# Spread one-hots made per batch between two message products, in a graph network layer on one core

## Chip, cores and metric

The kernel runs on one core of a Trainium2 chip. The metric is the device time of one execution in microseconds. A core has five instruction queues: PE (matmuls; PEld is its weight load), DVE (vector), ACT (scalar), POOL (which here issues the gathers) and SP (which only issues transfers). Each queue runs its instructions in the order written; semaphores hold an instruction until what it needs is done.

## The reference

One message passing layer with 1250 nodes of 512 features (a vector part of 3 x 128 and a scalar part of 128) and 40000 edges, sorted by their target node, followed by a residual sum and a layer norm:

```
s_j        = silu(x[src, 384:] @ W1 + b1) @ W3 + b3            # per edge, 384 wide
edge_basis = (rbf(r) * cutoff(r)) @ W2 + b2                     # 20 radial functions
s1, s2, s3 = split(s_j * edge_basis)                            # 128 each
v_msg      = v_j * s1[:, :, None] + s3[:, :, None] * edge_attr[:, None, :]
x          = x + segment_sum(concat(v_msg, s2), dst)
...        # per node: v@U, v@U@V, norms, a two-layer network, products -> rows
x          = x + segment_sum(rows[src], dst)
out        = layernorm(x0 + x)
```

The change concerns the term `s3 * edge_attr`: three vector components of an edge are the same 128 numbers, each times one of the edge's three attributes.

## The kernel before

**Tiles.** Edges come in 79 chunks of 512. A group is four chunks (16 tiles of 128 edges); there are 20 groups. A batch is one tile of each of the four chunks of a group: 4 batches a group, 80 batches, numbered t, with t = 4g + i. The last group is not full: its batches have 3, 2, 2 and 2 tiles. The targets of a chunk lie in a window of 32 nodes, so summing edges into nodes is a matmul with a one-hot matrix of 128 edges x 32 nodes. `hot` (line 759) has these one-hots of a group. `spread` (line 769) has each one-hot three times, times the edge's three attributes, so that `s3 * edge_attr` is summed by matmuls and never formed.

**A step of the main loop** (lines 1352 to 1370; step t):

- `messages(t)` (line 813): DVE multiplies the gathered table rows with the edge factors `eb`, which lie in PSUM: line 819 makes the part for s2 and s3 (1024 elements a partition for four tiles), line 820 the vector part (1536). The result `msg` has two buffers.
- `make_pair(t)` (line 834): DVE compares, for the count of links that the second sum needs.
- `run(first, t)`: single tasks of PE and ACT.
- `add_messages(t - 1)` (lines 851, 858): PE sums batch t-1 into `agg`, 4 matmuls with `hot` and 12 with `spread` (each recorded as two). `count_links(t - 1)` (line 876) follows.
- `run(early, t)`, then `edge_factors(t + 1)` (line 806): PE makes `eb` of the next batch in PSUM. There is one `eb` buffer, so this waits for line 820 of batch t.
- `gather(t + 3)` (line 700): POOL issues one indirect DMA for each tile, 128 rows of 2560 bytes. The first of them is also made to wait for `edge_factors(t + 1)`. Four `rows_t` buffers.
- `run(late, t)`, then `run(dve, t)`: single tasks of DVE, in an order set by a table.

The tables `first`, `early`, `late` and `dve` are written by hand, by step and rank; they repeat every eight steps (two groups). The tasks on DVE behind the pair are, by t mod 8 in the repeating part:

| t mod 8 | DVE tasks behind the pair, by line |
|---|---|
| 0 | 1046, 1052 (scaled rows of a node block), 911 (counts) |
| 1 | 948, 953 (sums of a block), 732 (basis arguments) |
| 2 | 920, 925 (counts), 761 (`make_hot`), 743 (`make_basis`) |
| 3 | 774 (`make_spread`), 743 |
| 4 | 774, 958 (residual), 911 |
| 5 | 1070 (a part of a row), 761, 722 (basis arguments) |
| 6 | 774, 1067 (a part of a row) |
| 7 | 774, 920, 925, 728 (basis arguments) |

Each line 774 makes half a group's spread: 8 tiles x 3 x 32 = 768 elements a partition. A group's spread has two buffers of 16 tiles. The first group's two halves are made in step 0 behind the pair.

**Around the loop.** Before it, node features are loaded, the table for the gathers is computed and written, and the edges' data are turned; the first gather starts 33 us into the span. While the loop runs, blocks of nodes whose sums are complete go through the second half of the layer, and PE begins products of the second sum (line 1118). The last L819 starts at 461.8 us; then the second sum and the layer norm are finished.

Of the kernel before, what the change touches and what calls it, by code (L numbers as in the profile page):

```python
# [10 lines left out]
F32 = mybir.dt.float32  # L11
# [9 lines left out]
P = 128  # L21
# [14 lines left out]
CPG = 4  # L36
SHARE = 16
MARGIN = 8
WIN = SHARE + 2 * MARGIN
# [23 lines left out]
def gnn_resnorm(  # L63
# [276 lines left out]
    with tc.If(misses_v == 0) as in_windows:  # L340
        windowed(tc, sh)
# [199 lines left out]
def windowed(tc, sh):  # L541
# [14 lines left out]
    NB, NGR, NCH, width = sh.NB, sh.NGR, sh.NCH, sh.width  # L556
# [4 lines left out]
    EPG = TPC * CPG  # L561
# [4 lines left out]
    def lanes(g, i, j):  # L566

        c = g * CPG + j
        if c >= NCH:
            return 0  # L570
        n = CHUNK if c < NCH - 1 else last_rows
        return max(0, min(P, n - i * P))


    batches = [(g, i) for g in range(NGR) for i in range(TPC) if lanes(g, i, 0)]
    NT = len(batches)

    def tiles(g, i):
        return [j for j in range(CPG) if lanes(g, i, j)]

    def runs(g, i):

        out = []
        for j in tiles(g, i):
            if out and lanes(g, i, out[-1][-1]) == lanes(g, i, j):
                out[-1].append(j)
            else:
                out.append([j])
        return [(slice(js[0], js[-1] + 1), len(js), lanes(g, i, js[0])) for js in out]
# [4 lines left out]
    def last_tile(g, j):  # L594
        return max(i for i in range(TPC) if lanes(g, i, j))
# [14 lines left out]
    with tc.tile_pool(name="msg", bufs=4) as pool, tc.tile_pool(  # L610
        name="rbf", bufs=1
# [77 lines left out]
        rows_of, msgs, onehots, turned, hots, spread = {}, {}, {}, {}, {}, {}  # L689
# [76 lines left out]
            )  # L766
            hots[g] = hot

        def make_spread(g, half):
            if half == 0:  # L770
                spread[g] = pool.tile([P, EPG, 3, WIN], F32, name="spread", bufs=2)
            n = EPG // 2
            at = slice(half * n, (half + 1) * n)
            nc.vector.tensor_mul(  # L774
                spread[g][:, at],
                hots[g][:, at, None, :].to_broadcast([P, n, 3, WIN]),
                sh.attr[:, g, at, :, None].to_broadcast([P, n, 3, WIN]),
            )
# [22 lines left out]
        def edge_factors(t):  # L801
            g, i = batches[t]
            eb = ps_work.tile([P, CPG, BANK], F32, name="eb")
            for j in tiles(g, i):
                rows = slice(j * FEAT, j * FEAT + N_RBF + 1)
                made = nc.tensor.matmul(  # L806
                    eb[:, j, :V], turned[g][rows, i, :], sh.w2_sb[rows, :],
                    start=True, stop=True,
                )
            ebs[t] = eb  # L810
            return made

        def messages(t):
            g, i = batches[t]
            eb, rows_t = ebs.pop(t), rows_of.pop(t)

            msg = pool.tile([P, CPG, V + 2 * C], F32, name="msg", bufs=2)
            for js, n, m in runs(g, i):
                nc.vector.tensor_mul(msg[:m, js, V:], rows_t[:m, js, V:], eb[:m, js, C:V])  # L819
                nc.vector.tensor_mul(  # L820
                    msg[:m, js, :V].rearrange("p t (k c) -> p t k c", k=3),
                    rows_t[:m, js, :V].rearrange("p t (k c) -> p t k c", k=3),
                    eb[:m, js, None, :C].to_broadcast([m, n, 3, C]),
                )
            msgs[t] = msg

        def make_pair(t):

            g, i = batches[t]
            pair = pool.tile([P, CPG, PARTS * WIN], F16, name="pair", bufs=2)  # L830
            for js, n, m in runs(g, i):
                e = g * EPG + i * CPG + js.start
                shape = [m, n, PARTS * WIN // 2, 2]
                nc.vector.tensor_tensor(  # L834
                    pair[:m, js, :].rearrange("p t (l h) -> p t l h", h=2),
                    number[:m, : PARTS * WIN].rearrange("p (l h) -> p l h", h=2)[
                        :, None
                    ].to_broadcast(shape),
                    column[:m, e : e + n, None, :].to_broadcast(shape),
                    op=ALU.is_equal,  # L840
                )
            pairs[t] = pair

        def add_messages(t):
            g, i = batches[t]
            if i == 0:
                aggs[g] = ps_sum.tile([P, width], F32, name="agg")
            agg, msg, js = aggs[g], msgs.pop(t), tiles(g, i)
            for j in js:
                m = lanes(g, i, j)  # L850
                nc.tensor.matmul(  # L851
                    agg[j * WIN : (j + 1) * WIN, :], hots[g][:m, i * CPG + j, :],
                    msg[:m, j, :width], start=(i == 0), stop=False, skip_group_check=True,
                )
            for c in range(3):
                for j in js:
                    m = lanes(g, i, j)
                    nc.tensor.matmul(  # L858
                        agg[j * WIN : (j + 1) * WIN, c * C : (c + 1) * C],
                        spread[g][:m, i * CPG + j, c, :], msg[:m, j, width:],  # L860
                        start=False, stop=(i == last_tile(g, j) and c == 2),
                        skip_group_check=True,
                    )

        def count_links(t):

            g, i = batches[t]
            if i == 0:
                adjs[g] = ps_sum.tile([P, BANK], F32, name="adj")
            adj, one, pair, js = adjs[g], onehots.pop(t), pairs.pop(t), tiles(g, i)  # L870
            to = adj[:, : PARTS * REACH].rearrange("s (p n) -> s p n", n=REACH)
            for j in js:
                m = lanes(g, i, j)
                at = j * SHARE

                nc.tensor.matmul(  # L876
                    to[:, :, at : at + WIN], one[:m, j, :],
                    pair[:m, j, :].rearrange("e (p n) -> e p n", n=WIN),
                    start=(i == 0 and j == js[0]), stop=(i == last_tile(g, j)),
                    skip_group_check=True,  # L880
                )
# [292 lines left out]
        first, early, late, dve = {}, {}, {}, {}  # L1174

        def at(when, step, rank, fn, *args):
            when.setdefault(step, []).append((rank, fn, args))
# [11 lines left out]
        for g in range(1, NGR, 2):  # L1189
            base, n = 4 * g - 4, min(2, NGR - g)  # L1190
            at(dve, max(0, base - 3), 4, make_turns, g, n, 0)
            at(dve, max(0, base - 1), 6, make_turns, g, n, 1)
            at(dve, base + 1, 6, make_turns, g, n, 2)
            at(dve, base + 1, 6, make_turns, g, n, 3)
            at(dve, base + 2, 4, make_hot, g)
            at(dve, base + 2, 5, make_basis, g)
            at(first, base + 3, 1, turn_basis, g)
            at(dve, base + 3, 2, make_spread, g, 0)
            at(dve, base + 4, 2, make_spread, g, 1)
            if n > 1:  # L1200
                at(dve, base + 3, 4, make_basis, g + 1)
                at(early, base + 5, 1, turn_basis, g + 1)
                at(dve, base + 5, 3, make_hot, g + 1)
                at(dve, base + 6, 2, make_spread, g + 1, 0)
                at(dve, base + 7, 2, make_spread, g + 1, 1)


        begins, ends = [], {}
# [78 lines left out]
        def run(when, step):  # L1287
            for _, fn, args in sorted(when.get(step, []), key=lambda task: task[0]):
                fn(*args)
# [18 lines left out]
        with tc.tile_pool(name="ps_rows", bufs=1, space=PSUM) as ps_rows:  # L1308
            beside = {0: number_sources, 2: turn_sources}
            for b in range(NB):  # L1310
                if b % 4 == 0:
                    name, bufs = (("rows_t", ROWS), ("msg", 2), ("msg", 2))[b // 4]
# [39 lines left out]
        for t in range(max(*first, *early, *late, *dve) + 1):  # L1352
            if t < NT:
                messages(t)
            if t < NT:
                make_pair(t)
            if t == 0:
                make_spread(0, 0)
                make_spread(0, 1)
            run(first, t)  # L1360
            if 1 <= t <= NT:
                add_messages(t - 1)
                count_links(t - 1)
            run(early, t)
            if t + 1 < NT:
                made = edge_factors(t + 1)
            if t + ahead < NT:
                gather(t + ahead, made)
            run(late, t)
            run(dve, t)  # L1370
# [367 lines left out]
```

## Time and profile before

| | |
|---|---|
| median of three executions | 522.23 us (518.22 to 525.12) |
| profiled execution: its time, its span | 523.57 us, 521.7 us |
| mean granted TensorE clock | 0.929 |
| busy of the span: PE, DVE, ACT, POOL | 83%, 83%, 71%, 68% |
| line 700, gathers | 313 of 1027 ns mean |
| line 819 / line 820 | 81 instructions each, 95.8 / 137.1 us |
| line 774, spread | 40 of 952 ns, 38.0 us |
| line 834, pair | 81, 38.4 us |
| line 858, matmuls with spread | 73.8 us |
| DMA, mean over the span | 239 GB/s, 124.93 MB |

A group of the profile is one line's instructions of one shape: how many, their busy time, the mean of one, then the idle time of the engine ahead of them and what ended it. A line of a view of waits gives the waiting instruction, what released it, the total in us, how often, and the longest. A line of the timeline gives the start and the duration in us, the engine, the line, the operation, what it writes from what, and in brackets the idle time ahead of it.

### The profile page before, as it was taken

The page shows a single profiled execution, that of the slowest core. Times are in us where ns is not written, and L with a number is a line of the kernel's source. Part 1 is how long each engine was busy: PE and PEld are TensorE (multiplying, and loading weights), DVE is VectorE, ACT ScalarE, POOL GpSimd, SP SyncE. Part 2 cuts the span into 40 slices and gives each one's busy share as a digit, 9 for nine tenths or more (in the row PEclk, how much of TensorE's full clock was granted, in tenths as well). Part 3 has the DMA queues.
Part 4 walks back from the last instruction along what each step waited for, and adds up shares of the span by engine and source line. Part 5 has one row for each costly group of instructions (what it writes and reads, how often), then busy time and mean ns, then how long its engine had stood idle before and what let it go on. Part 6 is the DMA issues. An engine that isn't in the chain of part 4 may idle for free.

```text
span 521.7 us, 11209 instructions
## 1 busy us (share of the span) xinstructions
PE 434.7 (83%) x4318; PEld 228.2 (44%) x4318; DVE 434.7 (83%) x588; ACT 369.1 (71%) x923; POOL 352.2 (68%) x359
## 2 busy tenths in 40 slices
PE   3864777788797979896899899899899899999993
PEld 2431333444354445454445345445445455456441
DVE  6698987979899999899898898899899789853391
ACT  1345775659788789779858788778887598844272
POOL 6437777777777777777777777777777767408300
PEclk9866888879988998899999999899999799999997
DMA  8668788887878888788888888888888878793032
GB/s 243 197 213 255 240 254 248 249 252 228 262 227 281 257 254 268 237 249 268 263 265 255 284 274 248 273 273 254 297 267 259 284 225 280 217 349 124 1 122 83
DMA packets 37166, 124.93 MB, mean 239 GB/s; under 512 B 6526, under 2 KB 8076, under 8 KB 37102
## 3 DMA queue, kind: packets, MB, share of 16 engines
q0 software_dynamic: 26016, 104.86, 65.6%
q1 hardware_dynamic: 9754, 18.61, 9.9%
q10 hardware_dynamic: 1332, 0.64, 0.4%
q8 instruction: 36, 0.59, 0.4%
q14 instruction: 28, 0.23, 0.1%
HBM read 112.48 MB, written 11.60 MB: 238 GB/s over the span
## 4 chain that ended last, share of the span: by engine, by line
PE 36%; DMA 25%; POOL 17%; DVE 11%; issue 9%; ACT 1%; DVEq 0%; POOLq 0%; ACTq 0%
DMA rows_t<-table,src_i 19%; POOL rows_t L700 15%; PE agg L851 7%; PE eb L806 5%; DVE msg L820 5%; PE agg L858 4%; DMA wu_sb<-in_L_gnn_Wu_dram 4%; DVE msg L819 4%; PE begun L1118 4%; PE adj L876 2%; PE work L1003 2%; PE adj L1118 2%; PE work L941 2%; PE eb L1118 2%; DMA store<-in_x_dram 1%
## 5 line engine op out<-in xcount | busy, mean ns | idle before, releaser
L700 POOL DMA_INDIRECT rows_t<-table,src_i x313 | 321.6, 1027 | 113.0 <-issue 74.4
L820 DVE TENSOR_TENSOR msg<-rows_t,eb 128x1536 f32<-128x1536 f32 (+1 forms) x81 | 137.1, 1693 | 0.0
L819 DVE TENSOR_TENSOR msg<-rows_t,eb 128x1024 f32<-128x1024 f32 (+1 forms) x81 | 95.8, 1183 | 45.1 <-DMA rows_t<-table,src_i 19.7
L796 ACT ACTIVATE one<-one,weight,src_f 128x128 f16<-128x128 f16 x313 | 128.5, 482 | 0.5 <-DVE magic L680 0.2
L806 PE MATMUL eb<-w_sb,basis_t 21*128 21x384 f32 x626 | 78.1, 555 | 55.7 <-DVE msg L820 53.8
L786 ACT ACTIVATE one<-number,low 128x128 f16<-128x128 f16 x313 | 99.7, 392 | 4.3 <-PE adj L876 2.8
L851 PE MATMUL agg<-msg,hot 128*32 128x512 f32 x626 | 96.2, 672 | 0.0
L858 PEld LDWEIGHTS agg<-msg,spread 128*32 128x32 f32 x1878 | 60.6, 118 | 57.8 <-issue 56.7
L858 PE MATMUL agg<-msg,spread 128*32 128x128 f32 x1878 | 73.8, 288 | 0.0
L806 PEld LDWEIGHTS eb<-w_sb,basis_t 21*128 21x128 f32 x626 | 27.3, 189 | 75.6 <-issue 43.7
L1118 PEld LDWEIGHTS <-counts 128*128 128x128 f16 x300 | 28.6, 100 | 33.0 <-issue 10.1
L1118 PE MATMUL begun<-store,counts 128*128 128x512 bf16 x147 | 41.5, 392 | 0.0
L834 DVE TENSOR_TENSOR pair<-number,column 128x640 f16<-128x640 f16 (+1 forms) x81 | 38.4, 475 | 0.0
L774 DVE TENSOR_TENSOR spread<-hot,attr 128x768 f32<-128x768 f32 x40 | 38.0, 952 | 0.0
L876 PE MATMUL adj<-pair,one 128*128 128x160 f16 x313 | 36.6, 240 | 0.0
L757 ACT COPY basis_t<-work 128x512 f32<-128x512 f32 x20 | 11.7, 587 | 28.3 <-PE work L752 28.1
L876 PEld LDWEIGHTS <-one 128*128 128x128 f16 x313 | 20.4, 99 | 17.1 <-issue 15.2
L851 PEld LDWEIGHTS agg<-msg,hot 128*32 128x32 f32 x626 | 13.1, 112 | 33.4 <-issue 23.0
L1113 POOL TENSOR_TENSOR msg<-msg,rows_t 128x512 f32<-128x512 f32 x12 | 15.8, 1338 | 17.3 <-ACT x L1060 17.0
L941 PE MATMUL work<-sums,sel 128*128 128x512 f32 x40 | 21.0, 650 | 0.0
L734 ACT ACTIVATE turn<-turn 128x640 f32<-128x640 f32 (+1 forms) x11 | 7.6, 689 | 18.8 <-DVE turn L732 18.8
L752 PE MATMUL work<-ident,basis 128*128 128x128 f32 x80 | 13.4, 295 | 6.8 <-DVE basis L743 6.7
(172 smaller groups left out, 542.1 us busy)
## 6 DMA issues: line engine op xcount, KB each, us to landing
rows_t<-table,src_i POOLq DMA_INDIRECT x313
spilled<-begun SPq DMA_DIRECT2D x12, 256.0 KB, 4.5
resid<-both_x SPq DMA_DIRECT2D x10, 256.0 KB, 5.4
rows_t<-spilled SPq DMA_DIRECT2D x2, 1280.0 KB
msg<-resid SPq DMA_DIRECT2D x2, 1280.0 KB
out_dram<-msg SPq DMA_DIRECT2D x8, 256.0 KB, 2.0
table<-msg SPq DMA_DIRECT2D x6, 320.0 KB, 3.2
store<-in_x_dram POOLq DMA_DIRECT2D x2, 768.0 KB
```

Source lines behind the costliest of these rows:

```text
L700: got = nc.gpsimd.indirect_dma_start(out=rows_t[:n, j, :], out_offset=None, in_=sh.table1, in_offset=bass.IndirectOffsetOnAxis(ap=sh.src_i ...
L774: nc.vector.tensor_mul(spread[g][:, at], hots[g][:, at, None, :].to_broadcast([P, n, 3, WIN]), sh.attr[:, g, at, :, None].to_broadcast([P, ...
L786: nc.scalar.activation(onehots[t][:, j, :], number[:, :P], AF.Abs, bias=low[:, e : e + 1])
L796: nc.scalar.activation(one, one, AF.Relu, scale=less[:, e : e + 1], bias=worth[:, e : e + 1])
L806: made = nc.tensor.matmul(eb[:, j, :V], turned[g][rows, i, :], sh.w2_sb[rows, :], start=True, stop=True,)
L819: nc.vector.tensor_mul(msg[:m, js, V:], rows_t[:m, js, V:], eb[:m, js, C:V])
L820: nc.vector.tensor_mul(msg[:m, js, :V].rearrange("p t (k c) -> p t k c", k=3), rows_t[:m, js, :V].rearrange("p t (k c) -> p t k c", k=3), ...
L834: nc.vector.tensor_tensor(pair[:m, js, :].rearrange("p t (l h) -> p t l h", h=2), number[:m, : PARTS * WIN].rearrange("p (l h) -> p l h", ...
L851: nc.tensor.matmul(agg[j * WIN : (j + 1) * WIN, :], hots[g][:m, i * CPG + j, :], msg[:m, j, :width], start=(i == 0), stop=False, skip_grou ...
L858: nc.tensor.matmul(agg[j * WIN : (j + 1) * WIN, c * C : (c + 1) * C], spread[g][:m, i * CPG + j, c, :], msg[:m, j, width:], start=False, s ...
L876: nc.tensor.matmul(to[:, :, at : at + WIN], one[:m, j, :], pair[:m, j, :].rearrange("e (p n) -> e p n", n=WIN), start=(i == 0 and j == js[ ...
L1118: nc.tensor.matmul(acc, counts[:, a, b * P : (b + 1) * P], table2(a, k), start=(start and a == first and k == 0), stop=(stop and a == end ...
```

## The change

`make_spread` no longer makes half a group but one batch (four tiles, 384 elements a partition, fewer in the last group). It is called from `messages(t)` between line 819 and line 820 of the batch's first run of tiles, and it is taken out of the task table and out of step 0. The buffers are three of four tiles in place of two of sixteen.

```
-        def make_spread(g, half):
-            if half == 0:
-                spread[g] = pool.tile([P, EPG, 3, WIN], F32, name="spread", bufs=2)
-            n = EPG // 2
-            at = slice(half * n, (half + 1) * n)
+        def make_spread(t):
+            g, i = batches[t]
+            spread[t] = pool.tile([P, CPG, 3, WIN], F32, name="spread", bufs=3)
+            n = len(tiles(g, i))
+            at = slice(i * CPG, i * CPG + n)
             nc.vector.tensor_mul(
-                spread[g][:, at],
+                spread[t][:, :n],
                 hots[g][:, at, None, :].to_broadcast([P, n, 3, WIN]),
                 sh.attr[:, g, at, :, None].to_broadcast([P, n, 3, WIN]),
             )
...
-            for js, n, m in runs(g, i):
+            for k, (js, n, m) in enumerate(runs(g, i)):
                 nc.vector.tensor_mul(msg[:m, js, V:], rows_t[:m, js, V:], eb[:m, js, C:V])
+                if k == 0:
+                    make_spread(t)
                 nc.vector.tensor_mul(
                     msg[:m, js, :V].rearrange("p t (k c) -> p t k c", k=3),
...
-                        spread[g][:m, i * CPG + j, c, :], msg[:m, j, width:],
+                        spread[t][:m, j, c, :], msg[:m, j, width:],
...
-            at(dve, base + 3, 2, make_spread, g, 0)
-            at(dve, base + 4, 2, make_spread, g, 1)
             if n > 1:
...
-                at(dve, base + 6, 2, make_spread, g + 1, 0)
-                at(dve, base + 7, 2, make_spread, g + 1, 1)
...
-            if t == 0:
-                make_spread(0, 0)
-                make_spread(0, 1)
             run(first, t)
```

## The prediction, made before the changed kernel was run

> **What bounds the kernel now.** I read the page first, then the chain that ended last, the waits of POOL, DVE and PE in the stretch of the batches (45 to 465 us), and last the timeline of single batches.
>
> ```profile
> span 521.7 us, 11209 instructions
> PE 434.7 (83%) x4318; PEld 228.2 (44%) x4318; DVE 434.7 (83%) x588; ACT 369.1 (71%) x923; POOL 352.2 (68%) x359
> PE 36%; DMA 25%; POOL 17%; DVE 11%; issue 9%; ACT 1%; DVEq 0%; POOLq 0%; ACTq 0%
> L700 POOL DMA_INDIRECT rows_t<-table,src_i x313 | 321.6, 1027 | 113.0 <-issue 74.4
> ```
>
> No engine is busy all the time, and POOL looks idle for a third of the span. That is misleading: the next view shows that its idle time between gathers is a fixed 0.3 us of issue.
>
> ```profile
> POOL rows_t L700 <- issue: 72.5, 238, 0.3
> POOL rows_t L700 <- PE eb L806: 5.2, 3, 2.0
> DVE msg L819 <- DMA rows_t<-table,src_i: 19.7, 31, 2.3
> PE eb L806 <- DVE msg L820: 53.8, 44, 6.0
> ```
>
> An undisturbed gather takes 0.95 us and 0.30 us of issue follow: one each 1.25 us, so 4 x 1.25 = 5.0 us a batch. Gathers run without a break from 33.05 to 453.97 us: 420.9 us for 313, of which 313 x 1.25 = 391 us are this pace. POOL waited for edge factors only three times. So the gather queue sets the pace of the batches (5.3 us on average from 48 to 446 us), and DVE (line 819) and PE wait behind it. What is above the pace is mostly hidden inside gathers: 297 of them start between 48 and 446 us, 76 lasted longer than 0.96 us, and together they lost 23.8 us. The timeline shows to what:
>
> ```profile
> 209.43 0.95 POOL L700 DMA_INDIRECT rows_t<-table,src_i  x1 [0.30 <-issue]
> 210.13 0.48 DVE L834 TENSOR_TENSOR pair<-number,column 128x640 f16<-128x640 f16 x1
> 210.53 0.95 DVE L774 TENSOR_TENSOR spread<-hot,attr 128x768 f32<-128x768 f32 x1
> 210.68 1.72 POOL L700 DMA_INDIRECT rows_t<-table,src_i  x1 [0.30 <-issue]
> ...
> 212.47 1.22 DVE L819 TENSOR_TENSOR msg<-rows_t,eb 128x1024 f32<-128x1024 f32 x1 [0.19 <-DMA rows_t<-table,src_i]
> 212.70 0.95 POOL L700 DMA_INDIRECT rows_t<-table,src_i  x1 [0.30 <-issue]
> ...
> 213.61 1.75 DVE L820 TENSOR_TENSOR msg<-rows_t,eb 128x1536 f32<-128x1536 f32 x1
> 213.95 0.95 POOL L700 DMA_INDIRECT rows_t<-table,src_i  x1 [0.30 <-issue]
> ```
>
> The gather at 210.68 started inside a spread and ended 0.92 us after it; those inside the two message products took the plain 0.95. Over the whole stretch all 76 stretched gathers end 0.74 to 0.94 us (mostly 0.82) after the end of a DVE instruction whose inputs all lie in SBUF (lines 722, 732, 743, 761, 774, 834, 920, 958, 1046, 1052, 1067, 1070), and none of the 161 gathers whose request fell into line 819 or 820, which read PSUM, is longer. I read this as a request 0.13 us (0.95 - 0.82) after a gather's start that such a DVE instruction holds up until it ends. Line 774 ended 23 of the waits, 11.1 us of the 23.8.
>
> **The change, part by part.**
>
> ```profile
> L774 DVE TENSOR_TENSOR spread<-hot,attr 128x768 f32<-128x768 f32 x40 | 38.0, 952 | 0.0
> L1052 DVE TENSOR_TENSOR square<-x,vv 128x384 f32<-128x384 f32 x10 | 5.6, 560 | 0.4
> ```
>
> Removed: 40 spreads of 0.952 us. Instructions on DVE overlap by some 0.08 us (line 820 starts 1.14 us after a line 819 of 1.22), so each occupies 0.87: 34.8 us. Added: 76 spreads of 384 elements and four at the end of 288 and 192. Line 1052 has that size and both inputs in SBUF: 0.56 us, 0.475 occupied. 76 x 0.475 + about 1.2 = 37.3 us. So DVE works 2.5 us more in 80 batches, below its idle time ahead of line 819 (45 us on the page): zero, at most +2.5. Three quarter-size buffers in place of two: the spread of batch t overwrites that of t-3, while line 819 of t already waits for the aggregation of t-2 (two msg buffers), so no new wait. Nothing on SP, and no DMA moves.
>
> Moved, first effect: line 820, the edge factors (PE, line 806) and the pair come 0.475 us later after line 819. PE idled for line 820 44 times and takes this as more idle time. The gathers of batch t+3 need the edge factors of t+1. I subtracted the end of line 806 from the moment when POOL came to them: mostly 2 to 4 us are left. In six or seven steps less than 1 us is left, and in nearly all of these PE itself was late by 0.5 us or more, so line 820 is not what counts. Bounds -1 and +3 us; I take 0. At the start two spreads (1.8 us) leave step 0, where 2.7 us of such slack hide them: 0. In the last batch the spread stands before the last product: +0.3.
>
> Second effect: steps even out badly. Of each eight steps four (t mod 8 = 3, 4, 6, 7) held a half spread after the pair; they become 0.39 us shorter. The others, 0, 1, 2 and 5, already of 4.7 to 5.15 us, become 5.1 to 5.6. The mean is 4.9, still below 5.3: DVE follows POOL on average, and I take 0; the bound is a rival below.
>
> Third effect, the one that I price: where DVE's SBUF instructions meet the requests. Measured from the start of line 819, the new spread lies at 1.14 to 1.70, line 820 reaches 3.36, and the pair is at 3.28 to 3.76 (now 2.80 to 3.28). When rows set the pace, line 819 starts 3.3 us after the end of its batch's last gather. A request comes 1.25 us after the last one was served, and its gather ends 0.82 us after it is served. I followed eight steps by hand with the rows' durations, from the state that repeats. Step 2: requests at 1.34 (in the spread, waits 0.36), 2.95, 4.20 (in line 761, 0.55); the gather served at 1.70 ends its batch, so the next step begins at 1.70 + 0.82 + 3.3 = 5.82. Step 3: 0.19, 1.44 (spread, 0.26), 2.95, 4.20 (line 743, 0.17). Step 4: 1.05, 2.30, 3.55 (pair, 0.21), 5.00. Step 5: 1.09, 2.34, 3.59 (pair, 0.17), 5.01 (line 722, 0.70). Step 6: 0.53 in spread and line 1067; step 7: 0.21 in the pair; step 0: 0.16 in the pair; step 1: 0.48 in the pair and line 732. Sum 3.81 us for eight steps, 0.48 a step. Measured now, by step 0 to 7: 0.19, 0.10, 0.31, 0.55, 0.32, 0.37, 0.42, 0.33, together 2.59, or 0.32 a step. (The same following on the present order gives 2.3 to 2.6, so the method is good to 0.3 in 2.6.) The long spreads' waits of 0.4 to 0.8 us go, but a short one in every step, plus the pair moved under a request, give more back: +0.16 us a step.
>
> That holds where rows set the step: in 40 of 76 line 819 started within 3.6 us of its last gather. In the other 36, disturbed by PE or by slower landings, a request falls anywhere: an instruction of d us then costs d x d / (2 x 1.25). That adds 0.125 for each new spread and removes 0.30 in every second step: -0.026 a step.
>
> Sum: 40 x 0.16 = +6.4, 36 x -0.026 = -0.9, last batch +0.3: +5.8 us. Profiled execution 523.57 (span 521.7) becomes 529.4; it lay 1.3 us above the median 522.23, so the median becomes 528.0. Bounds: -11.1 if all waits at spreads vanish and none arise; +12.2 if all 76 steps settle into the pattern.
>
> The Trainium skill, page "SBUF — State Buffer", section "SBUF: two separate sides", has VectorE and GpSimd share a port pair as an exclusive lock: whichever starts first holds it and the other fully blocks. The first half agrees with the 0.82 us above; the second would hold up DVE too, and is the fourth rival.
>
> **The rivals.** First, *the pattern settles everywhere*, also where landings disturb it: +9 to +14 us, 534. For it: a delayed request restarts the clock at an instruction's end, which locks the two engines together. Against: line 819's waits on rows, 31 in 81, are far from all.
>
> Second, the other side, *the spread hides between requests*. If requests fall at about 1.0 and 2.25 after line 819, as in steps 24, 26, 29 and 34 now, a spread at 1.14 to 1.70 meets none. Then the 11.1 us go, and the pair's waits, some 0.2 us in half the steps (+7.6), and 0.5 us in each of the nine steps of kind 5 come back: between -11 and +1, say 517. It decides if fewer than a third of the new spreads hold up a gather; the hand-followed pattern has three of eight.
>
> Third, *DVE becomes the bound*: steps 0, 1, 2 and 5 grow by 0.475 and the lighter steps win nothing back: 38 x 0.475 = +18 us, 540. For it: after 320 us many steps have no idle on DVE. Against: rows are fetched three batches ahead, and PE's edge factors start late there.
>
> Fourth, *DVE is held by a gather*: a gather has 0.82 of each 1.25 us, so a spread would wait 0.66 x 0.41 = 0.27 us, 20 us in 76, half of it (heavy steps) on the path on top of the sum: 538. Against: line 774 now takes 945 to 958 ns in all 40, also at 194.24, inside a gather that ran from 193.44 to 194.39.
>
> **How the numbers follow.** Forecast 0.49 (+2 to +9 us; 524 to 531), first rival 0.17, second 0.26, third 0.05, fourth 0.03. About 2% (10.4 us) is what a measurement of this kernel can tell from no change. Slower by more: half to two thirds of the first, third and fourth, the forecast's tail: 0.23. Faster by more: only the second's far end, 0.05. Within: 0.72. The range takes in the sum, most of the second rival, and the first: 517 to 538.
>
> **What would show it.** Line 774: 80 instructions, 0.56 us each at full size, DVE busy up by some 6 us (by durations). Gathers of line 700: mean up from 1027 ns to 1045 or so, some 30 of them ending 0.82 us after a spread, some 30 after the pair. POOL's waits on line 806 about the same; PE's on line 820 up by 15 to 20 us. The forecast is wrong if the gathers' mean stays or falls, or if the time between line 819's starts grows while the gathers' mean does not.

## The result, and the profile after

The changed kernel takes 523.46 us (median of 21 runs, 519.3 to 528.3) against 520.0 us before (median of 21 runs, with the three known before): a ratio of 1.0064, 95% interval 1.0045 to 1.0084. It is slower by two thirds of a percent, some 3.4 us. The forecast was +5.8 us on 522.23.

These are lines of the page of the profile after (523.46 us, so at its median). A line number above 820 is two higher than before.

```profile
span 521.7 us, 11214 instructions
PE 430.0 (82%) x4280; PEld 227.9 (44%) x4318; DVE 436.0 (84%) x628; ACT 368.9 (71%) x923; POOL 352.3 (68%) x359
PE 29%; DVE 24%; DMA 21%; POOL 13%; issue 10%; ACT 1%; DVEq 0%; POOLq 0%; ACTq 0%
L700 POOL DMA_INDIRECT rows_t<-table,src_i x313 | 321.4, 1027 | 110.3 <-issue 73.4
L819 DVE TENSOR_TENSOR msg<-rows_t,eb 128x1024 f32<-128x1024 f32 (+1 forms) x81 | 95.6, 1180 | 44.3 <-PE eb L806 19.1
L774 DVE TENSOR_TENSOR spread<-hot,attr 128x384 f32<-128x384 f32 (+2 forms) x80 | 43.4, 542 | 0.0
```

Gathers have the same mean as in the first profile, 1027 ns, and the span is the same. That pair hides the loss: the profiled execution before was 3.6 us slower than its kernel's median. What changed is who sits on the chain that ended last: DVE has 24% of it where it had 11%. And line 819 now waits for edge factors more than for rows (from 45 to 465 us 19.1 us in 21 waits against 16.9 in 16; before it was 9.6 in 7 against 19.7 in 31). The waits of POOL and PE from 45 us on (total, times, longest) are nearly the same as before:

```profile
POOL rows_t L700 <- PE eb L806: 7.0, 6, 1.9
PE eb L806 <- DVE msg L822: 53.0, 44, 6.4
```

The timeline of step 34 (t mod 8 = 2) shows what is new:

```profile
226.81 0.48 DVE L836 TENSOR_TENSOR pair<-number,column 128x640 f16<-128x640 f16 x1
227.21 0.32 DVE L922 COPY counts<-both 128x640 f16<-128x640 f16 x1
227.44 0.23 DVE L927 TENSOR_TENSOR counts<-counts,both 128x160 f16<-128x160 f16 x1
227.60 0.68 DVE L761 TENSOR_TENSOR hot<-lane,local 128x512 f32<-128x512 f32 x1
227.60 2.05 POOL L700 DMA_INDIRECT rows_t<-table,src_i  x1 [0.30 <-issue]
228.20 0.67 DVE L743 TENSOR_TENSOR basis<-turn,fade 128x320 f32<-128x320 f32 x1
228.79 1.21 DVE L819 TENSOR_TENSOR msg<-rows_t,eb 128x1024 f32<-128x1024 f32 x1
229.92 0.55 DVE L774 TENSOR_TENSOR spread<-hot,attr 128x384 f32<-128x384 f32 x1
229.95 1.34 POOL L700 DMA_INDIRECT rows_t<-table,src_i  x1 [0.30 <-issue]
```

The gather at 227.60 takes 2.05 us in place of 0.95: its request (0.13 us after its start) falls into line 761, is not served at the end of that line, where line 743 follows on, and is served only when line 743 ends. DVE has no idle ahead of line 819. The gather at 229.95 then waits 0.39 us for the spread. This wait of 1.1 us is in seven of the ten such steps of the first profile after and in eight of ten of a second one (523.23 us), always with the request 4.18 to 4.20 us after line 819. By the instruction that the wait ended behind, from 48 to 446 us, the first profile before and the first after have: at spreads 11.1 us in 23 gathers, then 7.4 in 37; at line 743 2.8 in 9, then 8.6 in 14; at the pair 2.4 in 14, then 3.9 in 18; in all 23.8, then 24.5.

### The profile page after: what moved, and what is told of

The parts are those of the page before. It is cut to its first block, busy times and chain, and to the rows that moved or that the text cites. A ratio compares the mean times of both kernels' runs of the same rounds, so it can differ in the third digit from the quotient of the medians.

```text
span 521.7 us, 11214 instructions
## 1 busy us (share of the span) xinstructions
PE 430.0 (82%) x4280; PEld 227.9 (44%) x4318; DVE 436.0 (84%) x628; ACT 368.9 (71%) x923; POOL 352.3 (68%) x359
## 3 DMA queue, kind: packets, MB, share of 16 engines
q1 hardware_dynamic: 9754, 18.61, 10.2%
## 4 chain that ended last, share of the span: by engine, by line
PE 29%; DVE 24%; DMA 21%; POOL 13%; issue 10%; ACT 1%; DVEq 0%; POOLq 0%; ACTq 0%
DMA rows_t<-table,src_i 16%; POOL rows_t L700 12%; DVE msg L822 8%; DVE msg L819 6%; PE agg L853 5%; PE eb L806 5%; DMA wu_sb<-in_L_gnn_Wu_dram 3%; PE agg L860 3%; PE begun L1120 3%; DVE spread L774 3%; PE adj L1120 2%; DMA store<-in_x_dram 2%; PE eb L1120 2%; PE adj L878 1%; DVE pair L836 1%
## 5 line engine op out<-in xcount | busy, mean ns | idle before, releaser
L700 POOL DMA_INDIRECT rows_t<-table,src_i x313 | 321.4, 1027 | 110.3 <-issue 73.4
L819 DVE TENSOR_TENSOR msg<-rows_t,eb 128x1024 f32<-128x1024 f32 (+1 forms) x81 | 95.6, 1180 | 44.3 <-PE eb L806 19.1
L806 PEld LDWEIGHTS eb<-w_sb,basis_t 21*128 21x128 f32 x626 | 27.6, 191 | 74.9 <-issue 45.5
L774 DVE TENSOR_TENSOR spread<-hot,attr 128x384 f32<-128x384 f32 (+2 forms) x80 | 43.4, 542 | 0.0
L1120 PE MATMUL begun<-store,counts 128*128 128x512 bf16 x113 | 33.4, 384 | 3.4 <-issue 2.4
L1115 POOL TENSOR_TENSOR msg<-msg,rows_t 128x512 f32<-128x512 f32 x12 | 15.8, 1339 | 17.2 <-PE work L1005 16.9
L943 PE MATMUL work<-sums,sel 128*128 128x512 f32 x40 | 19.8, 617 | 0.0
```

Of the source, the lines that this page charges most:

```text
L700: got = nc.gpsimd.indirect_dma_start(out=rows_t[:n, j, :], out_offset=None, in_=sh.table1, in_offset=bass.IndirectOffsetOnAxis(ap=sh.src_i ...
L774: nc.vector.tensor_mul(spread[t][:, :n], hots[g][:, at, None, :].to_broadcast([P, n, 3, WIN]), sh.attr[:, g, at, :, None].to_broadcast([P, ...
L806: made = nc.tensor.matmul(eb[:, j, :V], turned[g][rows, i, :], sh.w2_sb[rows, :], start=True, stop=True,)
L1120: nc.tensor.matmul(acc, counts[:, a, b * P : (b + 1) * P], table2(a, k), start=(start and a == first and k == 0), stop=(stop and a == end ...
```

## The experiments

Three theories were put against each other. *Hold*: gathers are stretched by DVE instructions that read SBUF alone, and that stretch is the time. *Load*: the change makes four steps of eight heavier, and DVE can't hide them. *Lateness* (and *granularity*): the vector product and the edge factors come later, or 80 small instructions cost more than 40. "Stretch" is the sum, over all 313 gathers of a profiled execution, of the duration beyond 0.947 us, that is, of what gathers lose inside their own durations. An expectation's "kind 2" is a step with t mod 8 = 2.

**The spread behind the pair**, small as in the change:

```
             for k, (js, n, m) in enumerate(runs(g, i)):
...
-                if k == 0:
-                    make_spread(t)
...
                 make_pair(t)
+                make_spread(t)
```

> The changed kernel with its per-batch spread moved behind the pair: the same 80 small spreads and the same load of each step, but the vector product, the edge factors and the pair are no longer 0.47 us later. Lateness theory (the loss comes from the later vector product, through the edge factors): as fast as before, ratio 1.000 +- 0.002. Load theory (the loss comes from the four heavy steps of eight, which DVE can't hide): as slow as the change, ratio 1.005 to 1.008. Hold theory (the loss comes from gathers held up by DVE instructions that read SBUF only): the time follows the stretch of the gathers, which was 23.8 us before and 24.5 us after; pair, spread and the next task now form one block, so some 22 to 27 us of stretch and a ratio of 0.997 to 1.006.

Measured: 523.94 us, ratio 1.0088 (1.0053 to 1.0122). As slow as the change, although nothing is late. The lateness theory falls, and with it the place between the two products as the cause. The time lies where the load theory had it and above the range of the hold theory (0.997 to 1.006), although the stretch of its profile, 24.4 us in an execution of 519.52 us, lies within what that theory expected.

**The old half-group spreads between the two products**, in the same steps as before:

```
-            at(dve, base + 3, 2, make_spread, g, 0)
+            at(between, base + 3, 2, make_spread, g, 0)
...                                   # the three others likewise
                 nc.vector.tensor_mul(msg[:m, js, V:], rows_t[:m, js, V:], eb[:m, js, C:V])
+                if k == 0:
+                    run(between, t)
```

> The kernel before with its 38 half-group spreads (768 elements) put between the two products of the same steps: instructions and loads of the steps as before, only the place changes, and the vector product is 0.87 us later in four steps of eight. Lateness theory: slower, ratio 1.005 to 1.010. Load theory: ratio 1.000 +- 0.002. Hold theory: a spread of 0.95 us between the products meets a request in about three of four cases (0.87 of 1.25 us) and costs 0.3 to 0.4 us each time, 9 to 12 us against 11.1 us before, while the block behind the pair gets shorter: stretch 20 to 25 us, ratio 0.995 to 1.002.

Measured: 520.83 us, 1.0018 (0.9988 to 1.0049): the vector product comes 0.87 us later in four steps of eight and nothing that can be told from no change is lost. Its profile (517.79 us) has 20.7 us of stretch.

**One more DVE instruction between the products**, from PSUM and from SBUF, in the kernel before:

```
                 nc.vector.tensor_mul(msg[:m, js, V:], rows_t[:m, js, V:], eb[:m, js, C:V])
+                if k == 0:
+                    nc.vector.tensor_mul(spare, rows_t[..., : 3 * WIN], eb[..., : 3 * WIN])   # from PSUM
+                    nc.vector.tensor_mul(spare, hots[g][...], sh.attr[...])          # or: from SBUF alone
```

> The kernel before with one more DVE instruction of 384 elements between the two products of every batch, which multiplies table rows with edge factors in PSUM into a buffer that nothing reads: the delay of the changed kernel without a second SBUF input, and some 37 us more work on DVE (nothing is taken away for it). DVE's mean step grows from 4.85 to 5.35 us, the pace of the gathers. Hold theory: the sum of the gathers' stretch stays at 20 to 25 us, none ends behind the new instruction. Lateness theory: ratio 1.005 to 1.015. Load theory: ratio 1.01 to 1.04, the heavy steps (5.6 us) show.

> As the run with the extra instruction from PSUM, but the extra instruction multiplies two SBUF operands (a second spread of the batch into a buffer that nothing reads). DVE's work is within 0.05 us a step of that run. Hold theory: 25 to 40 gathers end 0.82 us behind the new instruction, their stretch grows by 5 to 9 us, and the time is up to as much above the run with PSUM, less where DVE already sets the pace. Lateness and load theories: the same time as the run with PSUM, within 0.3%.

Measured: 534.61 us, 1.0295 (1.0252 to 1.0337), and 536.15 us, 1.0331 (1.0290 to 1.0373). The load costs as the load theory said, but the stretch did not stay at 20 to 25 us in the run with PSUM: it was 39.1 us, 14.7 of it at line 743. In the run from SBUF 32 gathers ended behind the new instruction (8.7 us), but the total is 40.7 us and the difference of the two times is not clear of noise. With more work on DVE, gathers are stretched at its other instructions. So load and hold are not rivals: in these two runs the load costs what the table below shows as stretch.

**Load alone and granularity alone.** In the first kernel the half-group spreads of before move into the heavy steps; in the second they stay, but each is issued as two instructions of 384 elements:

```
-            at(dve, base + 3, 2, make_spread, g, 0)
+            at(dve, base + 2, 6, make_spread, g, 0)
...                                   # + 4, + 6, + 7 become + 5, + 8, + 9
```

```
+            for first in (0, n // 2):
+                at = slice(half * n + first, half * n + first + n // 2)
                 nc.vector.tensor_mul(
-                spread[g][:, at],
+                    spread[g][:, at],
```

> The kernel before, its half-group spreads of 768 elements moved from steps 3, 4, 6 and 7 of eight to steps 2, 5, 0 and 1 behind the pair: same instructions, same place in a step, but the steps that have the other long tasks now grow by 0.87 us (to some 5.6 to 6.0 us of DVE work) where the change made them grow by 0.47. Load theory: about twice the loss of the change or more, ratio 1.010 to 1.030, and no idle on DVE in steps 0, 1, 2. Granularity theory (the loss comes from 80 small instructions in place of 40): ratio 1.000 +- 0.002. Hold theory: follows the gathers' stretch, which should stay within 20 to 30 us (-0.7% to +1.2%).

> The kernel before, each half-group spread issued as two instructions of 384 elements at the same place: the small instructions of the change (78 of them) without its shift of load between steps. Granularity theory: as slow as the change, ratio 1.005 to 1.008. Load theory: DVE works 0.09 us more in four light steps of eight, ratio 1.000 to 1.002. Hold theory: two short instructions back to back hold a gather like one long one, stretch 20 to 26 us, ratio 0.998 to 1.003.

Measured: 524.02 us, 1.0069 (1.0038 to 1.0100), and 520.49 us, 0.9980 (0.9945 to 1.0016). Granularity falls. The edit of the first kernel moves each half-group spread from a light step into a heavy one. Moving load into the four heavy steps costs as much as the change, though it moves twice as much; the size that I had expected of it (1.010 to 1.030) was too large.

**The spread with one SBUF input, and its control.** PE copies the batch's 12 attributes into unused columns of the edge factors' bank, and the spread reads them there. The control has the same matmul and does not use it:

```
+            nc.tensor.matmul(eb[:, 0, V : V + 3 * n], ident, sh.attr[:, g, ...], start=True, stop=True)
             ebs[t] = eb
...
-                sh.attr[:, g, at, :, None].to_broadcast([P, n, 3, WIN]),
+                eb[:, 0, V : V + 3 * n] ...to_broadcast([P, n, 3, WIN]),      # not in the control
```

> The changed kernel, in which PE puts the batch's 12 attributes into the unused columns of the edge factors' PSUM bank (one more small matmul a batch, behind the edge factors) and the spread reads them there, so that it has one SBUF input only. Hold theory: no gather waits for a spread any more, the 7.4 us of stretch at spreads go to zero, and the time falls by 3 to 7 us against the change, ratio to before 0.993 to 1.001. Load theory: DVE's load is as in the change, or a little more (a PSUM operand), so ratio 1.005 to 1.010, the matmul (0.2 to 0.3 us of PE a batch) included.

> The control for the attributes in PSUM: the changed kernel with the same extra matmul of each batch, but the spread reads its attributes from SBUF as in the change, so only the second SBUF input of the spread differs from that run. Hold theory: the gain goes, ratio to before 1.004 to 1.012, 25 to 40 gathers end 0.82 us behind a spread again. If the matmul itself had brought the gain (PE kept busy, or a shift of the edge factors), the ratio stays at 0.996 to 1.002.

Measured: 518.44 us, 0.9990 (0.9952 to 1.0029) with the attributes in PSUM; 526.77 us, 1.0110 (1.0069 to 1.0152) for the control. These are lines of the page of the first and then of the second:

```profile
L700 POOL DMA_INDIRECT rows_t<-table,src_i x313 | 318.4, 1017 | 110.7 <-issue 72.3
L774 DVE TENSOR_TENSOR spread<-hot,eb 128x384 f32<-128x384 f32 (+2 forms) x80 | 43.1, 538 | 0.0
```

```profile
L700 POOL DMA_INDIRECT rows_t<-table,src_i x313 | 323.5, 1033 | 114.2 <-issue 76.8
L774 DVE TENSOR_TENSOR spread<-hot,attr 128x384 f32<-128x384 f32 (+2 forms) x80 | 43.5, 544 | 0.0
```

DVE's spreads take the same time in both (538 and 544 ns); what differs is where one input lies. The gathers' mean falls by 16 ns, 5 us in 313, and the median time by 8.3 us. With PSUM no stretched gather ends behind a spread; in the control 30 do (8.3 us). In the control a gather that starts 0.08 us behind a spread lasts 1.29 us:

```profile
224.22 0.56 DVE L774 TENSOR_TENSOR spread<-hot,attr 128x384 f32<-128x384 f32 x1
224.30 1.29 POOL L700 DMA_INDIRECT rows_t<-table,src_i  x1 [0.31 <-DVE msg L825]
```

In the kernel with PSUM one that starts 0.08 us behind a spread runs unhindered:

```profile
221.46 0.55 DVE L774 TENSOR_TENSOR spread<-hot,eb 128x384 f32<-128x384 f32 x1
221.54 0.95 POOL L700 DMA_INDIRECT rows_t<-table,src_i  x1 [0.30 <-DVE msg L827]
221.93 1.75 DVE L830 TENSOR_TENSOR msg<-rows_t,eb 128x1536 f32<-128x1536 f32 x1
```

That the spread's second SBUF input holds the gathers is so shown. The whole 8.3 us is not: of the 9.6 us between the two profiled executions 5.5 are stretch, and 3.5 are idle time of POOL between gathers (110.7 and 114.2 us above). The granted TensorE clock differs too, 0.955 and 0.932 in the profiles, 0.947 and 0.935 as medians of the executions. Whether the clock is part of the cause here was not tried. The same question stands for the change itself, with a median clock of 0.931 where three sets of executions of the kernel before had 0.936 to 0.938.

**Relief of the heavy steps**, alone and together with the attributes in PSUM:

```
-            at(dve, base + 2, 4, make_hot, g)
+            at(dve, base + 3, 5, make_hot, g)
...
-                at(dve, base + 5, 3, make_hot, g + 1)
+                at(dve, base + 6, 3, make_hot, g + 1)
```

> The changed kernel with make_hot (0.69 us on DVE) moved from step 2 to step 3 and from step 5 to step 6 of eight, out of heavy steps into the ones that the change made light: DVE's work a step, now 5.1, 5.2, 5.3, 4.3, 4.8, 5.6, 4.3, 4.5 us for steps 0 to 7, becomes 5.1, 5.2, 4.7, 4.9, 4.8, 5.0, 4.9, 4.5. Load theory: most of the loss comes back, ratio to before 0.996 to 1.003. Hold theory: the wait of 1.1 us at lines 761 and 743 in every step 2 (10 us in the changed kernel's profile) becomes some 0.3 us, stretch falls to 15 to 20 us and the time by 4 to 8 us. Granularity theory: as the change, 1.005 to 1.008.

> The changed kernel with both reliefs: the spread's attributes read from PSUM, and make_hot moved from steps 2 and 5 to steps 3 and 6 of eight. Hold theory (the time is the gathers' pace plus their stretch): no gather waits for a spread, and the long waits at lines 761 and 743 shrink; stretch 13 to 19 us where the two reliefs alone had 20.9 and 20.6, and a ratio to before of 0.985 to 0.997. Load theory: the heavy steps are gone, but holds don't count: 0.998 to 1.004, as with make_hot moved alone.

Measured: 521.57 us, 1.0030 (1.0004 to 1.0057) alone: about half of the loss comes back, though the interval touches that of the change; its profile (517.64 us) has 22.3 us of stretch, somewhat more than the 15 to 20 expected. Together: 516.28 us, 0.9932 (0.9890 to 0.9973), faster than both kernels. The gathers' mean is then 1009 ns:

```profile
L700 POOL DMA_INDIRECT rows_t<-table,src_i x313 | 316.0, 1009 | 111.7 <-issue 74.0
```

**Further profiles of the two kernels.**

> The kernel before, profiled once more, since its profiled execution (523.57 us) lay 3.6 us above its median of 520.0 us, while that of the change lay at its median. Hold theory: in an execution near 520 us the sum of the gathers' stretch is 20 to 22 us where the first profile had 23.8, and the execution's time less the stretch is the same 499 to 501 us as in the other profiles. Load theory: stretch and time are unrelated.

> The changed kernel, profiled once more. Hold theory: the execution's time less the stretch of the gathers is 498 to 501 us again; stretch near 24 to 25 us if the execution lies near 523.5 us, with the wait of 1.1 us in most steps of kind 2.

Measured: 524.21 us with 27.0 us of stretch before, 523.23 us with 27.1 us after. Neither profile of the kernel before fell near its median of 520 us, so they can't tell how much stretch an execution at the median has. Four more profiles of before and two of the change were taken for it:

> The kernel before, profiled a third time. Hold theory: its time is 495 to 499 us plus the stretch of all gathers; if it lies at 519 to 521 us the stretch is 21 to 24 us (25.8 and 27.0 in the two at 523.6 and 524.2 us). If the stretch is 25 to 27 us at 520 us, the loss of the change in the timed runs is not stretch.

> The kernel before, profiled a fourth time, with the same expectation: stretch of all gathers 21 to 24 us where the time is 519 to 521 us, 25 to 27 us where it is 523 to 525 us.

> The changed kernel, profiled a third time. Hold theory: time less stretch 495 to 499 us, stretch of all gathers 25 to 28 us at 522 to 525 us, and the wait of 1.1 us at lines 761 and 743 in most of the nine steps of kind 2.

> The kernel before, profiled again. Hold theory: 495 to 499 us plus the stretch of all gathers; stretch 21 to 24 us where the time is 519 to 521 us, 25 to 27 us where it is 523 to 525 us. If the stretch is 25 to 27 us at 520 us, the loss of the change in the timed runs is not stretch.

> The kernel before, profiled again, with the same expectation as the run before it.

> The changed kernel, profiled again. Hold theory: stretch of all gathers 25 to 28 us at 522 to 525 us, with the wait of 1.1 us at lines 761 and 743 in most of the nine steps of kind 2.

They came from two other chips, on which either kernel needs 610 to 619 us: 610.1 and 610.7 us before and 611.3 after on the one, 619.2 and 618.5 before and 614.1 after on the other. There POOL waits ahead of most batches, above all for edge factors, as its waits in the third profile before show:

```profile
POOL rows_t L700 <- PE eb L806: 57.3, 26, 4.1
```

There stretch is 9.7 to 10.2 us before and 22.6 to 24.1 us after, and the times do not follow it: the change has 12 to 14 us more stretch and is some 1 us slower on the one chip, 4 to 5 us faster on the other. That a stretched gather only shortens the next wait would explain this, but was not tested, and these are three executions a chip. Why the chips are slower stays open. The profiles show where the mechanism ends: where POOL waits ahead of most batches, stretch does not set the time.

**The profiles together.** These are the ones at the usual pace:

| kernel | profiled execution, us | stretch, us | difference |
|---|---|---|---|
| both reliefs | 516.3 | 20.2 | 496.1 |
| make_hot later | 517.6 | 22.3 | 495.3 |
| half spreads between | 517.8 | 20.7 | 497.1 |
| attributes in PSUM | 518.1 | 22.1 | 496.0 |
| spread behind the pair | 519.5 | 24.4 | 495.1 |
| after, two profiles | 523.5; 523.2 | 25.5; 27.1 | 498.0; 496.1 |
| before, two profiles | 523.6; 524.2 | 25.8; 27.0 | 497.8; 497.2 |
| halves in heavy steps | 523.3 | 26.5 | 496.8 |
| matmul only | 527.7 | 27.6 | 500.1 |
| extra from PSUM; from SBUF | 532.9; 535.0 | 39.1; 40.7 | 493.8; 494.3 |

The times differ by 19 us, the times less stretch by 6; without the two kernels with an extra instruction it is 11 and 5. So most of what one kernel's execution is slower than another's goes with gathers held up. One profile is left out of the table: the split spreads', an execution of 526.3 us, 5.8 above that kernel's median. It has 24.1 us of stretch, so a difference of 502.2, more than any in the table.

## Why the prediction was right or wrong

**Right: the bound and the mechanism.** POOL's gathers set the pace, and DVE's instructions that read SBUF alone hold them up. This was inferred from one trace and is now shown by taking the second SBUF input away, with a control: 30 gathers held behind a spread, then none (ratios 1.0110 and 0.9990). The Trainium skill, page "SBUF — State Buffer", section "SBUF: two separate sides", says that a VectorE instruction with two SBUF inputs contends for a port pair that GpSimd shares, though only against a GpSimd operation that reads SBUF; for these gathers the runs show such a hold. The same section says that the loser fully blocks, whichever it is. For DVE no run shows that: line 774 took at most 604 ns in the first profile after, where its median was 551, so a gather costs a spread some 0.05 us at most and not 0.8. The fourth rival was wrong, as forecast.

**Right: no new cost of lateness.** I took 0 for the later edge factors; POOL's wait on line 806 went from 5.2 to 7.0 us, within my bounds, and the two kernels that separate place from load agree (1.0088 without lateness, 1.0018 with it). My expectation that PE's wait for the vector product would grow by 15 to 20 us was wrong: it is 53.0 us after 53.8. PE's idle time in a paced loop is the loop's time less PE's work, and neither changed much.

**Wrong: the size of the third term, 40 x 0.16 = 6.4 us.** I followed eight steps to a sum of 3.81 us of waits. Measured in the first profile after: 24.5 us in 74 steps, 2.65 us for eight. The prediction's own sign of being wrong came too: the gathers' mean stayed at 1027 ns. By step, forecast and measured: step 0 0.16 and 0.10; 1 0.48 and 0.19; 2 0.92 and 1.00; 3 0.43 and 0.39; 4 0.21 and 0.23; 5 0.87 and 0.31; 6 0.53 and 0.14; 7 0.21 and 0.21. Five are close, and the three that are not are 1, 5 and 6. Step 2 is close by luck: I had 0.36 us at the spread and 0.55 at line 761, and measured were some 0.16 at the spread and 0.83 at lines 761 and 743. In step 5 I let a request at 5.01 us wait 0.70 us for line 722; in the four steps of that kind where it came at 5.01 or 5.02 it waited at most 0.08 us. In three of the four the gather started within 0.02 us of line 722 and was served at once, and line 722 took 0.85 to 0.87 us in place of 0.81. Without that wait the request of step 6 mostly misses the spread. In step 1 the requests mostly come at 2.9 and 4.2 us, ahead of line 732, since the step before is set by DVE and not by rows. So the new stretch of this pair of profiles is +0.7 us and not +5.5.

**Wrong: the second term, the uneven steps, taken as 0.** Steps 0, 1 and 2 now mostly take 5.17 to 5.25 us with no idle on DVE, within the 5.1 to 5.6 us that the prediction gave the heavy steps. I compared DVE's mean, 4.9 us, with the pace, and concluded that DVE follows. But three heavy steps in a row set their own pace and lock the requests to DVE: in most steps with t mod 8 = 2 (kind 2) one falls at 4.19 us and waits 1.1 us, where I had 0.55 for it. Stretch in steps of kind 2 went from 3.1 to 10.0 us, while that of steps 3 to 7 fell from 18.0 to 11.6. The runs bear it out: load moved into these steps without any small spread costs as much as the change (1.0069), load taken out of them alone ends at 1.0030, and with the spread's hold gone as well at 0.9932.

So two steps of the prediction failed: the third term was mis-sized (6.4 less 0.9 us of new stretch, measured +0.7), and the uneven steps, put at 0, cost as much as the change when they alone are made uneven. In this pair of profiles the stretch is the sum of a gain and a loss of nearly equal size: long spreads no longer hold up gathers in light steps (-6.4 us), and heavy steps hold them up more (+6.9). That the time still moved the forecast way, by 3.4 us where 5.8 were forecast, is luck as far as these profiles show: the term that was to make it did not. What stays open is where 3.4 us lie in a typical pair of executions: both usable profiles before were 3.6 to 4.2 us slower than that kernel's median, with 25.8 and 27.0 us of stretch, as much as after. By the table an execution at 520 us would have some 23 us; none of the kernel before was profiled. That the load of the heavy steps is the cause is shown; that it costs its time as stretch in a typical execution is not.

## What to carry to other kernels

When one queue sets the pace, look inside its instructions: a duration that varies where the work does not is a wait, and the ends of what ran beside it tell for what it waited. Price a moved instruction by what it holds up and by the step that it makes the longest, not by the mean load of its engine. And before giving a small effect to a pair of profiles, see how far each execution lies from its kernel's median.

## What the runs showed of the hardware

A gather that waits is not always served between two DVE instructions that follow each other. In the first profile before, requests 0.55 to 0.77 us ahead of a spread's end were served at that end, although the next SBUF instruction followed on; a request 0.55 us ahead of line 761's end, in the change, waited through line 743 too, 1.1 us. The same happened once in the first profile before, to a request 0.35 us ahead of a spread's end (0.90 us, through line 743). What decides that was not tried.

Nor does every request that falls into such an instruction wait. In the first profile after there were 94, at least 0.08 us ahead of the end of a DVE instruction with all inputs in SBUF. Held were 75; the 19 that were not all came within 0.15 us of that instruction's start, so their gathers had started at most 0.02 us behind it (though some that came as early were held). Where the request of such a gather came 0.11 to 0.15 us behind the start, the DVE instruction was the one that lasted longer: spreads took 0.57 to 0.60 us in place of 0.55.
